# Moving the second copy of a hidden-layer chain and pair 0's attention in a hand-ordered two-layer graph kernel

## The chip, the cores and the metric

The kernel runs on one core of a Trainium2 chip. A core has a matrix engine (TensorE, PE in the profile), a vector engine (VectorE, DVE), an activation engine (ScalarE, ACT), a general engine (GpSimd, POOL) and a queue engine that issues DMA transfers (SyncE, SP). Each engine takes its own instructions in the order in which the program lists them, and waits at an instruction until its inputs are there. The metric is the device time of one execution in microseconds (us); lower is better.

## What is computed

There are 128 graphs of 128 nodes with 512 features each (`x`), and a 128 x 128 adjacency matrix for each graph (`adj`). Two layers follow, each with a residual and a layer norm. All arithmetic is float32. Cut to what matters:

```python
# layer 0: graph attention, 8 heads of 64 units
feats = einsum('bnf,hfu->bhnu', X, W)
e_self, e_neigh = feats . a_self, feats . a_neigh
dense = leaky_relu(e_self[..., :, None] + e_neigh[..., None, :], 0.2)
dense = dense + NEG_BIG * (1.0 - A)
att = softmax(dense)
x = layernorm(x + relu(att @ feats + b))
# layer 1: hypergraph convolution, 512 -> 1024 -> 512, twice
#   conv(x, W, b) = D^-1 H B^-1 H^T (x @ W^T) + b
h = layer_norm(relu(conv(x, W1, b1)), gamma, beta)
x = layernorm(x + conv(h, W2, b2) + x)
```

## The kernel before

The graphs are taken two at a time: 64 pairs, `p` = 0 to 63, with the two graphs `g` = 0 and 1 of a pair handled together. For the large products the kernel treats the two graphs and the two halves of the features as a 2 x 2 block matrix and forms it from seven half-size products instead of eight. `chain` (line 325 on) writes these out: products 1, 2, 6, 5, 7, 4, 3 in this order, into three PSUM banks called X, Y and W. Products 1, 6, 7 and 4 all add onto bank X, and its contents are needed at three stages, so ScalarE copies X out three times: copy 0 after product 1, copy 1 after product 6, copy 2 after product 7, ahead of product 4. A product that adds onto X can only start when the copy before it has read the bank. There are three such chains per pair: `pf` (attention features), `ph` (the hidden layer, 512 to 1024) and `py` (back to 512). The products of `ph` are at line 843 in the profile, those of `pf` and `py` at line 479, and all chain copies at line 335.

The order of all work is written by hand. Every step carries a due time. `at(lag, time, fn, ...)` and `@step(lag, time)` say that the step of pair `p` is due at `(p + lag) * T + time` with `T = 38.6`; the due times have no unit on the chip, they only order the program. A table `first` gives other due times for single steps of the first pairs, and a list `todo` holds the one-time preparations and pair 0's own steps. At the end everything is sorted by due time and issued in that order. So while one pair is in its `ph` chain (lag 3), the pair behind it is in its softmax (lag 2) and the one behind that in its feature products (lag 1).

ScalarE's part of that mixture matters here. In each period it runs, for the pair in the softmax, `leaky` (line 598, four instructions for half of one graph's heads) and `exponential` (line 612, likewise), and, for the pair ahead of it, the copies out of the `ph` chain. VectorE takes the row maximum between the two (`largest`, line 604), forms the sums of the chain (`h_sum`, line 858) and a skip term (`skip`, line 796). GpSimd does the mask (`masked`, line 582), the bias (`add_bias`, line 733), sums of blocks (`z_sums`, `h_sums`) and the power -0.5 of the variances (`rstds`, line 758).

Pair 0 goes through a prologue that differs from the other pairs. Its exponentials are transposed on TensorE (`e_transpose_first`, tile `pet`), evicted alternately by VectorE and ScalarE, and multiplied with the features by `attend` (line 670, tile `pav`), one block for each graph `g` and half of the heads `q`. `attended` (lines 706 and 707) divides by the softmax's denominator, `add_bias` adds the bias, `residual` (lines 742, 750 and 751) applies the relu, adds `x` and takes the statistics of a graph, `rstds` makes the inverse deviation from both graphs' statistics, and `first_shift` and `first_output` (lines 776 to 785) normalise. Only then can `propagate` (line 808, tile `pz`) start the second layer; it also needs `R`, which `r_evict` (line 443) makes. Besides, the prologue prepares weights: `prepare_hidden` (line 240) forms sums of 1024 columns for the hidden layer, three on GpSimd and one on VectorE. `prepare_output_spread` spreads one row over all partitions by a TensorE product (tile `gw`), and `prepare_output_blocks` (line 291, four instructions per block) scales the output weights with it on VectorE.

Of the kernel before, what the change touches and what calls it, by code (L numbers as in the profile page):

```python
# [20 lines left out]
def kernel(  # L21
# [45 lines left out]
    nc = tc.nc  # L67
# [21 lines left out]
    def bank(name):  # L89
        return psum.tile([P, HALF], F32, tag="bank", name=name)  # L90
# [223 lines left out]
    def at(lag, time, fn, *args, since=0, until=PAIRS):  # L314
        steps.append((lag, time, fn.__name__, range(since, until), fn, args))

    def chain(kind, lag, times, multiply, w, extra=0, since=0, until=PAIRS):

        tag = "chain" if w == HALF else "half"

        def product(p, s, i):
            where, start = {1: ("X", 1), 2: ("Y", 1), 6: ("X", 0), 5: ("W", 1), 7: ("X", 0),
                            4: ("X", 0), 3: ("W", 0)}[i]
            if start:
                s[kind, where] = bank(f"{kind}{where}_{p}")
            multiply(s, i, s[kind, where], start)  # L330

        def copy(p, s, i):
            n = w + (extra if i < 2 else 0)
            t = s[kind, i] = work.tile([P, HALF if w == HALF else FW], F32, tag=f"{tag}_{i}", name=f"{kind}{i}_{p}")
            nc.scalar.copy(t[:, :n], s[kind, "X"][:, :n])  # L335

        for i, t in zip((1, 2, 6, 5, 7, 4, 3), times):
            at(lag, t, product, i, since=since, until=until)
        for i, t in enumerate(times[7:]):
            at(lag, t, copy, i, since=since, until=until)  # L340
# [495 lines left out]
    def hidden(s, i, to, start):  # L836
# [4 lines left out]
        for m in range(KH // 2):  # L841
# [4 lines left out]
                    skip_group_check=True,  # L846
                )

    chain("ph", 3, (2.0, 3.8, 5.6, 7.35, 9.1, 12.65, 14.4, 4.0, 7.5, 11.0), hidden,
          HALF)  # L850

    def hid(s, g, q):
# [265 lines left out]
    for t, fn, *args in (  # L1118
# [21 lines left out]
        (15.46, load_weights, (nc.sync, w1_blocks[:1:-1], w1t, F // 2, HALF)),  # L1140
        (16.1, everywhere, (b2_bc, b2, nc.sync)),
        (79.0, prepare_hidden, (nc.gpsimd, 2)), (79.1, prepare_hidden, (nc.gpsimd, 0)),
        (79.2, prepare_hidden, (nc.gpsimd, 1)), (110.6, prepare_hidden, (nc.vector, 3)),
        (15.5, prepare_output_vectors, ()), (16.0, prepare_output, ()),
        (78.3, prepare_rows, ()), (78.79, prepare_output_sums, ()),
        (78.92, prepare_output_spread, (0, "gw")), (98.0, prepare_output_spread, (1, "bw")),
        (98.1, prepare_output_bias, ()), (98.2, prepare_output_blocks, (slice(0, 1),)),
        (99.75, prepare_output_blocks, (slice(1, 2),)),
        (117.8, prepare_output_blocks, (slice(2, 3),)),
# [14 lines left out]
        ("edges", 1): 110.4, ("scale_edges", 1): 110.5, ("neighbours", 1): 80.1,  # L1164
        ("propagator", 1): 117.76, ("spread_nodes", 1): 80.3, ("r_evict", 1): 121.8,
        ("leaky", 0, 1, 1): 77.65, ("leaky", 0, 0, 1): 73.6, ("largest", 0, 0, 1): 75.3,
        ("attend", 0, 0, 0): 78.95, ("attend", 0, 0, 1): 78.96, ("attend", 0): 97.85,
        ("attended", 0, 0): 99.7, ("attended", 0, 1): 99.8,
        ("leaky", 1, 0, 0): 117.85, ("leaky", 1, 0, 1): 117.9, ("leaky", 1, 1, 0): 119.9,
        ("largest", 1, 0, 0): 118.0, ("largest", 1, 0, 1): 118.2, ("largest", 1, 1, 0): 120.2,  # L1170
        ("masked", 1, 0, 0): 109.0, ("masked", 1, 1, 1): 121.5,
# [7 lines left out]
    for p, time, fn, *args in (  # L1179
        (0, 11.4, x_transpose_first), (0, 11.5, x_transpose_out, 0), (0, 11.5, x_transpose_out, 1),  # L1180
        (0, 12.5, plain_features, 0), (1, 12.55, x_transpose_first),
        (0, 12.6, plain_features, 1), (0, 12.65, adj_transpose_first),
        (0, 13.0, plain_features_out), (1, 13.1, x_transpose_out, 0), (1, 13.8, x_transpose_out, 1),
        (1, 14.5, plain_features, 0), (1, 14.6, plain_features, 1),
        (1, 15.6, plain_features_out), (1, 97.9, adj_transpose_first),
        (0, 78.8, e_transpose_first, 0, 0), (0, 78.85, e_transpose_first, 0, 1),
        (0, 78.9, e_transpose_first, 1, 0), (0, 79.3, e_transpose_first, 1, 1),
    ):
        todo.append((time, run, (fn, p, args)))
    for p in range(PAIRS):  # L1190
# [73 lines left out]
```

## Time and profile before

| | before |
|---|---|
| time, median of 3 runs | 2439.44 us (2438.86 to 2441.68) |
| span of the profiled execution | 2435.9 us |
| mean granted TensorE clock | 0.998 |
| TensorE matmul busy | 2408.6 us (99%) |
| VectorE busy | 1931.5 us (79%) |
| GpSimd busy | 1795.8 us (74%) |
| ScalarE busy | 1523.3 us (63%) |
| memory traffic | 140 GB/s over the span |

The span runs from the first to the last instruction; the time of a run is a little longer. Busy times are sums over instructions. A busy matmul engine is drawn with modelled ends, since matmuls overlap, so short gaps can disappear under them. In the lines of a timeline the first number is the start in us from the span's beginning, the second the length of a merged group of like instructions, then engine, source line, operation, output and inputs. A bracket at the end gives the idle time before the group and what is thought to have ended it. From about 90 us to 2380 us one pair follows another: the `propagate` products of consecutive pairs start 37.24 to 37.26 us apart from pair 2 on.

### The profile page before, as it was taken

The page shows a single profiled execution, that of the slowest core. Times are in us where ns is not written, and L with a number is a line of the kernel's source. Part 1 is how long each engine was busy: PE and PEld are TensorE (multiplying, and loading weights), DVE is VectorE, ACT ScalarE, POOL GpSimd, SP SyncE. Part 2 cuts the span into 40 slices and gives each one's busy share as a digit, 9 for nine tenths or more (in the row PEclk, how much of TensorE's full clock was granted, in tenths as well). Part 3 has the DMA queues.
Part 4 walks back from the last instruction along what each step waited for, and adds up shares of the span by engine and source line. Part 5 has one row for each costly group of instructions (what it writes and reads, how often), then busy time and mean ns, then how long its engine had stood idle before and what let it go on. Part 6 is the DMA issues. An engine that isn't in the chain of part 4 may idle for free.

```text
span 2435.9 us, 52769 instructions
## 1 busy us (share of the span) xinstructions
PE 2408.6 (99%) x18273; PEld 2148.9 (88%) x18273; DVE 1931.5 (79%) x4456; ACT 1523.3 (63%) x4481; POOL 1795.8 (74%) x2060
## 2 busy tenths in 40 slices
PE   7999999999999999999999999999999999999998
PEld 5898888998988988989989889889899898888897
DVE  7887788778878877887788788878877887887776
ACT  4665665765756656657557566576575675665763
POOL 5877777777777777777777777777777777777774
PEclk9999999999999999999999999999999999999999
DMA  6545545545455455454455555554544545545531
GB/s 185 140 145 146 146 136 148 153 131 150 138 142 149 143 145 147 134 155 141 133 147 148 140 145 147 145 147 131 157 137 135 153 140 145 144 142 150 147 110 53
DMA packets 432762, 345.30 MB, mean 142 GB/s; under 512 B 153176, under 2 KB 382064, under 8 KB 432496
## 3 DMA queue, kind: packets, MB, share of 16 engines
q1 hardware_dynamic: 429024, 337.46, 48.9%
q10 hardware_dynamic: 3472, 4.47, 0.6%
q8 instruction: 145, 2.38, 0.4%
q14 instruction: 121, 0.99, 0.1%
HBM read 239.08 MB, written 102.73 MB: 140 GB/s over the span
## 4 chain that ended last, share of the span: by engine, by line
PE 97%; DVE 1%; DMA 1%; ACT 1%; issue 0%; POOL 0%; SPq 0%; POOLq 0%; DVEq 0%; ACTq 0%
PE phX L843 19%; PE pyX L479 18%; PE phW L843 9%; PE pfX L479 9%; PE pyW L479 9%; PE pav L696 5%; PE pz L808 5%; PE phY L843 5%; PE pfW L479 5%; PE pq L1009 4%; PE pyY L479 4%; PE pfY L479 2%; PE pd L435 1%; PE pf L516 1%; PE py L1055 0%
## 5 line engine op out<-in xcount | busy, mean ns | idle before, releaser
L335 ACT COPY py<-pyX 128x257 f32<-128x257 f32 x189 | 70.9, 375 | 531.5 <-PE pyX L479 527.0
L843 PEld LDWEIGHTS phX<-zS,w_sb 128*128 128x128 f32 x3072 | 362.8, 192 | 41.5 <-issue 31.6
L843 PE MATMUL phX<-zS,w_sb 128*128 128x128 f32 x3072 | 378.9, 276 | 2.4 <-POOL xS L461 1.3
L896 POOL TENSOR_TENSOR sq<-sq 128x512 f32<-128x512 f32 (+2 forms) x384 | 326.4, 850 | 20.3 <-ACT sq L884 0.3
L582 POOL TENSOR_TENSOR nb<-nb,neg 128x512 f32<-128x512 f32 x256 | 318.0, 1275 | 7.6 <-DMA nb<-rd 7.2
L598 ACT ACTIVATE nb<-nb,ft 128x128 f32<-128x128 f32 x1020 | 317.3, 390 | 7.1 <-POOL nb L582 7.1
L758 POOL TENSOR_TENSOR rso<-veo,mhalf 128x2 f32<-128x2 f32 x63 | 44.1, 700 | 372.6 <-DVE veo L756 372.6
L612 ACT ACTIVATE nb<-nb,nm 128x128 f32<-128x128 f32 x1024 | 313.8, 394 | 0.4 <-DVE nm L604 0.4
L604 DVE TENSOR_REDUCE nm<-nb 128x4 f32<-128x512 f32 x256 | 172.5, 682 | 132.1 <-ACT nb L598 120.2
L873 ACT ACTIVATE h<-h,vecs 128x128 f32<-128x128 f32 x768 | 245.6, 395 | 34.6 <-DVE h L858 34.6
L479 PE MATMUL pyX<-w_sb,hS 128*128 128x257 f32 x1008 | 245.6, 385 | 0.0
L479 PE MATMUL pyX<-w_sb,h 128*128 128x257 f32 x1008 | 239.2, 379 | 0.5 <-ACT py L335 0.5
L479 PE MATMUL pyW<-w_sb,hS 128*128 128x256 f32 x1008 | 238.6, 378 | 1.0 <-DVE y L927 1.0
L479 PEld LDWEIGHTS pyX<-w_sb,h 128*128 128x128 f32 x1008 | 190.9, 190 | 29.0 <-ACT py L335 0.9
L479 PEld LDWEIGHTS pyW<-w_sb,hS 128*128 128x128 f32 x1008 | 190.6, 189 | 28.8 <-issue 1.4
L479 PEld LDWEIGHTS pyX<-w_sb,hS 128*128 128x128 f32 x1008 | 185.7, 189 | 28.7
L502 DVE TENSOR_TENSOR ft<-pf,pfW 128x264 f32<-128x264 f32 x124 | 53.3, 429 | 165.9 <-PE pfW L479 87.4
L633 DVE STREAM_TRANSPOSE eT<-eb 128x512 f32<-128x512 f32 x252 | 163.6, 687 | 2.5 <-DMA eb<-ed 2.1
L733 POOL TENSOR_TENSOR y<-y,b_bc 128x512 f32<-128x512 f32 x128 | 160.3, 1273 | 2.4 <-DVE y L707 1.1
L884 ACT ACTIVATE sq<-h 128x512 f32<-128x512 f32 x256 | 160.5, 628 | 2.1
L461 POOL TENSOR_TENSOR hS<-h 128x512 f32<-128x512 f32 x126 | 158.5, 1277 | 2.2 <-ACT h L873 2.2
L999 DVE SCALAR_TENSOR_TENSOR y<-y,rsh,bw_bc 128x512 f32<-128x512 f32 x126 | 148.3, 1215 | 11.7 <-POOL rsh L995 8.9
(178 smaller groups left out, 5687.7 us busy)
## 6 DMA issues: line engine op xcount, KB each, us to landing
nb<-rd SPq DMA_DIRECT2D x127, 512.0 KB
ed<-nb SPq DMA_DIRECT2D x126, 512.0 KB
eb<-ed SPq DMA_DIRECT2D x504, 128.0 KB
x<-in_x_dram SPq DMA_DIRECT2D x64, 512.0 KB
out_dram<-o SPq DMA_DIRECT2D x63, 512.0 KB
xb<-in_x_dram SPq DMA_DIRECT2D x248, 128.0 KB
a<-in_adj_dram SPq DMA_DIRECT2D x64, 128.0 KB
w<-in_adj_dram SPq DMA_DIRECT2D x128, 64.0 KB
```

Of the source, the lines that this page charges most:

```text
L461: engine.tensor_tensor(t[:, i], in0, in1, op=op)
L479: nc.tensor.matmul(to[:, :n], lhs[:, k, :], rhs[:, k, :n], start=bool(start) and k == 0, stop=(k == nk - 1), skip_group_check=True,)
L582: nc.gpsimd.tensor_tensor(t, t, neg[:, :, None, :].to_broadcast([P, NB, HH, B]), op=ALU.add)
L598: nc.scalar.activation(t, t, AF.Prelu, bias=s["ft"][:, g, h, 0:1], alpha=SLOPE)
L604: nc.vector.tensor_reduce(s["nm"][:, g, hs], scores(p, s, g, hs).rearrange("p b h j -> p h b j"), AX.XY, ALU.max, negate=True,)
L612: nc.scalar.activation(t, t, AF.Exp, bias=s["nm"][:, g, h:h + 1])
L633: nc.vector.transpose(s["eT"][:, g, hs, :].rearrange("p h (b i) -> p h b i", b=NB), s["eb", g][:, :, hs, :].rearrange("p b h j -> p h b j"),)
L733: nc.gpsimd.tensor_tensor(s["y"][:, g, :], s["y"][:, g, :], b0_bc, op=ALU.add)
L843: nc.tensor.matmul(to[:, m * N:(m + 1) * N], w[:, k, m * P:(m + 1) * P], rhs[:, k, :], start=bool(start) and m == 0 and k == 0, stop=(k == ...
L873: nc.scalar.activation(dst[:, k, :], src[:, k, :], AF.Relu, bias=b1_sb[:, c:c + 1])
L884: nc.scalar.activation(s["sq"][:, g, q * KH // 2:(q + 1) * KH // 2, :], hid(s, g, q), AF.Square, scale=DH ** -0.5,)
L896: nc.gpsimd.tensor_tensor(t[:, :n, :], t[:, :n, :], t[:, n:2 * n, :], op=ALU.add)
```

## The change

Three things are moved; no instruction is added or taken away.

The first edit is in the `ph` chain and so in every pair. Copy 1 is due at 5.95 in place of 7.5. The next pair's `leaky` for its second graph and second half of the heads is due at 6.0, so on ScalarE the copy now precedes it.

The second concerns TensorE, ScalarE and VectorE in the prologue. Pair 0's fourth transpose comes before the attention products, these follow for both graphs in a row, and the product that spreads `gw` comes behind them. The division, bias, residual and statistics of both graphs are due together, and the inverse deviation right after them. The second weight block and `R` come behind that.

The third is on GpSimd: the second sum of the hidden weights (`prepare_hidden` with index 1) is due after pair 0's two bias additions in place of before them.

The purpose is to have the copy that product 7 waits for done before other ScalarE work of another pair, and to bring pair 0's two graphs to the second layer side by side.

```diff
-    chain("ph", 3, (2.0, 3.8, 5.6, 7.35, 9.1, 12.65, 14.4, 4.0, 7.5, 11.0), hidden,
+    chain("ph", 3, (2.0, 3.8, 5.6, 7.35, 9.1, 12.65, 14.4, 4.0, 5.95, 11.0), hidden,
           HALF)
...
-        (79.2, prepare_hidden, (nc.gpsimd, 1)), (110.6, prepare_hidden, (nc.vector, 3)),
+        (98.0, prepare_hidden, (nc.gpsimd, 1)), (110.6, prepare_hidden, (nc.vector, 3)),
...
-        (78.92, prepare_output_spread, (0, "gw")), (98.0, prepare_output_spread, (1, "bw")),
+        (78.99, prepare_output_spread, (0, "gw")), (98.0, prepare_output_spread, (1, "bw")),
...
-        ("attend", 0, 0, 0): 78.95, ("attend", 0, 0, 1): 78.96, ("attend", 0): 97.85,
-        ("attended", 0, 0): 99.7, ("attended", 0, 1): 99.8,
+        ("attend", 0, 0, 0): 78.95, ("attend", 0, 0, 1): 78.96, ("attend", 0, 1, 0): 78.97,
+        ("attend", 0, 1, 1): 78.98, ("attended", 0, 0): 97.8, ("attended", 0, 1): 97.81,
+        ("add_bias", 0, 0): 97.82, ("add_bias", 0, 1): 97.83,
+        ("residual", 0, 0): 99.6, ("residual", 0, 1): 99.65, ("rstds", 0, "a"): 99.7,
...
-        (0, 78.9, e_transpose_first, 1, 0), (0, 79.3, e_transpose_first, 1, 1),
+        (0, 78.9, e_transpose_first, 1, 0), (0, 78.93, e_transpose_first, 1, 1),
```

## The prediction, made before the changed kernel ran

> **What bounds the kernel now.** I read the page first: the engine that is busy all the time, and the chain that ended last.
>
> ```profile
> PE 2408.6 (99%) x18273; PEld 2148.9 (88%) x18273; DVE 1931.5 (79%) x4456; ACT 1523.3 (63%) x4481; POOL 1795.8 (74%) x2060
> ...
> PE 97%; DVE 1%; DMA 1%; ACT 1%; issue 0%; POOL 0%; SPq 0%; POOLq 0%; DVEq 0%; ACTq 0%
> ```
>
> TensorE sets the end, so a faster helper engine is worth only what it takes out of TensorE's waits. Its idle time is 2435.9 - 2408.6 = 27 us, nearly all before 90 us and after 2380 us. But the change moves something in every pair, so I next read the timeline of one middle pair, TensorE first, then ScalarE.
>
> ```profile
> 1028.51 1.95 PE L843 MATMUL phX<-zS,w_sb 128*128 128x128 f32 x16
> 1030.30 1.95 PE L843 MATMUL phW<-zS,w_sb 128*128 128x128 f32 x16
> 1032.22 2.02 PE L843 MATMUL phX<-zS,w_sb 128*128 128x128 f32 x16
> 1034.08 1.89 PE L1009 MATMUL pq<-y,R 128*128 128x512 f32 x4
> ...
> 1027.99 2.45 ACT L612 ACTIVATE nb<-nb,nm 128x128 f32<-128x128 f32 x8
> 1030.34 1.27 ACT L598 ACTIVATE nb<-nb,ft 128x128 f32<-128x128 f32 x4
> 1031.51 0.57 ACT L335 COPY ph<-phX 128x512 f32<-128x512 f32 x1
> 1031.97 2.45 ACT L612 ACTIVATE nb<-nb,nm 128x128 f32<-128x128 f32 x8
> 1034.32 0.58 ACT L335 COPY ph<-phX 128x512 f32<-128x512 f32 x1
> ```
>
> The columns are start, length and group. From product 6 (1028.51) to product 5 (1030.30) is 1.79 us, as between any two full products here. From product 5 to product 7 it is 1.92. Product 7 adds onto bank X, which the second copy reads, and that copy ends at 1031.51 + 0.57 = 1032.08; product 7 starts 0.14 later. TensorE was ready at 1030.30 + 1.785 = 1032.085. So product 7 seems to wait 0.135 to 0.14 us for the copy's signal, in every pair. Going through the timeline pair by pair, the distance is 1.92 or 1.93 in all of pairs 1 to 62 (62 times). The last pair has no attention work left on ScalarE, and is the control:
>
> ```profile
> 2403.75 1.95 PE L843 MATMUL phW<-zS,w_sb 128*128 128x128 f32 x16
> 2405.53 1.95 PE L843 MATMUL phX<-zS,w_sb 128*128 128x128 f32 x16
> ...
> 2403.95 0.59 ACT L335 COPY ph<-phX 128x512 f32<-128x512 f32 x1 [3.21 <-PE phX L843]
> ```
>
> There the copy ends at 2404.54, early, and the distance is 1.78. In pair 0 product 7 starts at 62.30, again 0.71 after the copy's start at 61.59, as in the middle pair (1032.22 - 1031.51). So this is a wait, though the page books it as nothing.
>
> Third, the prologue, from the timelines and the windows view.
>
> ```profile
> 39.32 2.37 POOL L240 TENSOR_TENSOR w_sb<-w_sb 128x1024 f32<-128x1024 f32 x1
> 44.15 1.64 POOL L733 TENSOR_TENSOR y<-y,b_bc 128x512 f32<-128x512 f32 x1 [1.14 <-DVE y L707]
> 45.76 0.40 POOL L369 TENSOR_SCALAR neg<-a 128x256 f32<-128x256 f32 x1
> ...
> 45.82 0.88 DVE L742 SCALAR_TENSOR_TENSOR y<-y,x 128x512 f32<-128x512 f32 x1 [0.21 <-POOL y L733]
> 47.68 0.17 DVE L756 TENSOR_SCALAR vea<-mva 128x2 f32<-128x2 f32 x1
> ...
> 49.92 3.64 PE L808 MATMUL pz<-R,y 128*128 128x128 f32 x16 [7.18 <-ACT y L785]
> 65.58 2.02 PE L843 MATMUL phX<-zS,w_sb 128*128 128x128 f32 x16 [1.25 <-POOL xS L461]
> ...
> 63.73 1.28 ACT L612 ACTIVATE nb<-nb,nm 128x128 f32<-128x128 f32 x4 [0.40 <-DVE nm L604]
> 64.92 0.56 ACT L335 COPY ph<-phX 128x512 f32<-128x512 f32 x1
> ...
> 48.00:50.00 2.00, 0.08 (x1) 0.08 (x1) 1.90 (x8) 1.32 (x4) 2.00 (x3) 0.50 0.05 7
> ```
>
> TensorE waits 7.18 us for pair 0's normalised rows, then again at 65.58. That second wait is named for GpSimd, but product 4 follows the third copy of X: 64.92 + 0.56 = 65.48, plus about 0.1. That copy stands behind four exponentials, these behind the maximum that VectorE takes at 63.02. And VectorE is busy almost without a break from 38.33 to that maximum (18.82 of the 20 us from 40 to 60). VectorE, not TensorE, sets when pair 0 gets through.
>
> **What the Trainium skill says.** Perfetto Trace Analysis, "Tensor Engine Instruction (MATMUL, LD_WEIGHTS)": a matmul's reported end is estimated, and the travel of a semaphore is outside the window. The trace agrees: product 5 is drawn until 1032.25, past the start of its successor, so a 0.14 us bubble lies under a modelled tail. GPSIMD Engine Reference, "Key points": GpSimd shares its SBUF interfaces with VectorE and contends with instructions that have two SBUF inputs. The trace agrees: the residual at 45.82 ends 0.54 us after GpSimd's 0.40 us mask does (46.70, 46.16), where the one before it took 0.68 in all. So I treat a GpSimd instruction as holding such a VectorE instruction off until it ends. TensorE: Matmul & The Clock Gate, "What's actually happening": after an idle window of about 3.4 us the clock is halved, until it has been busy about as long. Here it stopped at 42.74 and shows 0.50 from 48 to 53.
>
> **Part 1, the second copy at 5.95 in place of 7.5.** In ScalarE's order it jumps ahead of the four leaky activations of the next pair, second graph, second half (due 6.0 of lag 2). Nothing is added or removed. The copy can start when the exponentials are out (1030.34) and product 6 has drained (1028.51 + 1.95 = 1030.46): 1030.5, ending 1031.05 instead of 1032.08. TensorE's 1032.085 is then 1 us away, and the wait goes: 62 x 0.14 = 8.7 us.
>
> The price: ScalarE now waits about 0.15 us for product 6, and behind the copy stand the leaky activations (0.6 later), eight exponentials (0.15 later) and the third copy. The third copy ends near 1035.05; product 4, due at 1035.66, hides it by 0.5. The last maximum on VectorE moves from 1031.89 to about 1032.2, and with it the sum over W (1035.88 to 1036.2, done by 1036.8), which must be read before product 3 at 1037.45: hidden by 0.6. VectorE stands idle 1.3 us at each feature sum, which absorbs the rest. The exponentials' write to DRAM leaves 0.15 later; the transposes that read it back find it early (only 2.1 us of waits on it in the run, 3 times). One of these 3 is the last pair's second graph, where VectorE and then TensorE (0.36 us at 2385.61) wait for it on the chain to the end. So pair 62 gains nothing and 0.15 is lost: 8.7 - 0.14 - 0.15 = 8.4 us.
>
> **Part 2, the prologue.** The fourth transpose of pair 0 goes ahead of attention, all four attention blocks follow it, then the gw row. TensorE: fourth transposes from 37.3 (exponentials end 37.15) to 37.8; attention at 0.54 each, to 40.0; gw ready at 41.1 (before: 38.3). VectorE: attended 0 from 38.5 to 39.6, attended 1 to 40.7 (before 41.0 and 44.0), 0.45 idle for gw, first weight block 41.15 to 42.7 (1.57). GpSimd: the second weight sum (2.37 us, at 39.32 above) moves behind both biases: bias 0 from 39.65 to 40.9, bias 1 to 42.2, weight sum to 44.55. Residual 0 is ready at 42.7, but it has two SBUF inputs, so I let it wait for the weight sum: 44.55. Then 1.6 us for each graph's residual and statistics: the variance at 47.9, against 47.68. Without the hold it would be 46.05. From the variance to pz is 2.24 us (49.92 - 47.68): pz at about 50.1. The second weight block (1.56) and R (0.33) that now follow the variance end at 49.8, just before y, so R delays nothing. DRAM row loads behind dnb start some 5 us later but are used after 57 us.
>
> From there VectorE has the same work as before, 1.9 us of it moved behind the variance. Its three two-port or two-input steps (hB twice, the last weight sum) again queue behind GpSimd's three masks, now 49.2 to 52.95; the last mask decides. I get the next maximum at 55.75 against 55.45, so product 4 and all behind it are 0.3 later. Moving copy 1 in pair 0 lets product 7 start near 60 instead of 62.3, and TensorE then only waits longer at product 4. Part 2: +0.3 us; if residual 0 is not held, the same steps give -1.5.
>
> **Sum.** 2439.44 - 8.4 + 0.3 = 2431.3 us.
>
> **Rivals.**
> A. Prologue also gains: residual 0 slips in ahead of the weight sum. For it: only 0.5 us decide. Against: the wait for gw. 2439.44 - 8.4 - 1.5 = 2429.5.
> B. The 0.14 us is eaten by another wait, at product 4, product 3 or a feature copy, whose slacks I read as 0.5, 0.6 and 0.3 us. For it: TensorE fed by three busy engines. Against: all three are at least twice the 0.14 us. Then 2439.44 + 0.3 = 2439.7, no change.
> C. Slower: the later maximum pushes VectorE's sums into TensorE by some 0.1 us per pair, 62 x 0.1 = 6.2, with the prologue's 0.3: 2446. Against: the idle 1.3 us twice per pair on VectorE.
>
> **How the numbers follow.** Forecast 0.60, A 0.24, B 0.10, C 0.06. The first two are faster by over 0.2% (4.9 us), and a partly eaten gain is too: 0.86. B gives most of same, 0.08; C slower, 0.06. The range takes in A with the scatter of the runs below (2428.6) and above the forecast a halved clock after the longer wait at product 4, or a quarter of the gain lost: 2434.6.
>
> **What would show it.** Product 5 to product 7 at 1.79 in all middle pairs, the pitch of pairs 37.25 to 37.11; the second copy straight behind the exponentials, with a short wait on TensorE. In the prologue: both attended groups done by 41, residual 0 starting late with a length near 2.4 us (right) or at 0.7 (rival A), pz near 50.1, product 4 near 65.9. I am wrong if the pitch stays at 37.25, whoever is then named.

## The result and the profile after

The changed kernel takes 2428.53 us (median of 4 runs, 2427.39 to 2428.98), beside 2439.93 for the kernel before: a ratio of 0.9952, with a 95% interval of [0.9935, 0.9969] (brackets behind a ratio are this interval from here on). The forecast was 2431.3, its range 2428.6 to 2434.6. So the direction was right, the time lies 0.07 us below the range, and the gain of 10.9 us against the forecast's 2439.44 came out a third larger than the 8.1 foreseen. The profiled span went from 2435.9 to 2425.6, that is by 10.3.

TensorE still sets the end. First the page of the kernel before, three groups that the prediction did not read: a line, an operation with count, then busy time and mean length, then the idle time ahead of it.

```profile
L843 PEld LDWEIGHTS phX<-zS,w_sb 128*128 128x128 f32 x3072 | 362.8, 192 | 41.5 <-issue 31.6
L843 PE MATMUL phX<-zS,w_sb 128*128 128x128 f32 x3072 | 378.9, 276 | 2.4 <-POOL xS L461 1.3
...
L999 DVE SCALAR_TENSOR_TENSOR y<-y,rsh,bw_bc 128x512 f32<-128x512 f32 x126 | 148.3, 1215 | 11.7 <-POOL rsh L995 8.9
```

The page of the changed kernel:

```profile
PE 2398.0 (99%) x18273; PEld 2140.8 (88%) x18273; DVE 1947.1 (80%) x4456; ACT 1519.0 (63%) x4481; POOL 1795.3 (74%) x2060
...
L843 PEld LDWEIGHTS phX<-zS,w_sb 128*128 128x128 f32 x3072 | 363.0, 192 | 33.0 <-issue 30.4
L843 PE MATMUL phX<-zS,w_sb 128*128 128x128 f32 x3072 | 374.3, 275 | 2.4 <-POOL xS L461 2.4
...
L999 DVE SCALAR_TENSOR_TENSOR y<-y,rsh,bw_bc 128x512 f32<-128x512 f32 x126 | 148.2, 1214 | 31.7 <-POOL rsh L995 31.4
```

Two things went and one came. The weight loads of products 6, 7 and 4 wait 41.5 - 33.0 = 8.5 us less: 62 times 0.137, the wait that the prediction found. Their matmuls are also busy 378.9 - 374.3 = 4.6 us less, 62 times 0.074, though not one of them was removed or made smaller: this the prediction did not foresee. And VectorE now waits 31.4 us in place of 8.9 for GpSimd's `rsh`, which has to do with a third term of the sum, taken up below.

The timeline of a middle pair after, TensorE and then ScalarE:

```profile
1024.74 1.95 PE L843 MATMUL phX<-zS,w_sb 128*128 128x128 f32 x16
1026.53 1.95 PE L843 MATMUL phW<-zS,w_sb 128*128 128x128 f32 x16
1028.31 1.95 PE L843 MATMUL phX<-zS,w_sb 128*128 128x128 f32 x16
1030.10 1.89 PE L1009 MATMUL pq<-y,R 128*128 128x512 f32 x4
...
1026.72 0.59 ACT L335 COPY ph<-phX 128x512 f32<-128x512 f32 x1
1027.21 1.28 ACT L598 ACTIVATE nb<-nb,ft 128x128 f32<-128x128 f32 x4
1028.39 2.45 ACT L612 ACTIVATE nb<-nb,nm 128x128 f32<-128x128 f32 x8
```

Copy 1 now precedes `leaky` and ends at 1027.31, a full microsecond before product 7. From product 5 to product 7 it is 1.78 (before 1.92), as forecast. From product 7 to `pq` it is 1.79 (before 1034.08 - 1032.22 = 1.86), and product 7 itself is drawn 1.95 long in place of 2.02.

The distance between the starts of consecutive groups, as a mean over pairs 2 to 61, accounts for the pitch, which is the distance from one pair's `pz` to the next pair's (worked out from the traces of both kernels, in us):

| from - to | before | after | difference |
|---|---|---|---|
| product 5 to product 7 (`ph`) | 1.925 | 1.787 | -0.138 |
| product 7 to `pq` | 1.860 | 1.787 | -0.073 |
| product 6 to product 5 (`pf`) | 0.890 | 0.912 | +0.022 |
| product 1 to product 2 (`ph`) | 1.787 | 1.799 | +0.012 |
| product 2 to product 6 (`pf`) | 0.890 | 0.892 | +0.002 |
| whole pitch | 37.254 | 37.080 | -0.175 (from means not rounded) |

Over the 60 pitches from pair 2 to pair 62 that is 10.47 us. Up to `pz` of pair 2 it takes 0.29 longer (128.90, before 128.61), and the last pitch is 32.33 in place of 32.48. So 0.29 - 10.47 - 0.15 = -10.33, the whole difference of the spans. The medians lie 0.6 us further down than that (10.9), less than the 2.8 us over which the runs of the kernel before scatter.

The prologue, GpSimd, VectorE and TensorE:

```profile
42.55 2.35 POOL L240 TENSOR_TENSOR w_sb<-w_sb 128x1024 f32<-128x1024 f32 x1
...
42.85 2.59 DVE L742 SCALAR_TENSOR_TENSOR y<-y,x 128x512 f32<-128x512 f32 x1
46.30 0.66 DVE L742 SCALAR_TENSOR_TENSOR y<-y,x 128x512 f32<-128x512 f32 x1
47.94 0.17 DVE L756 TENSOR_SCALAR vea<-mva 128x2 f32<-128x2 f32 x1
...
50.17 3.78 PE L808 MATMUL pz<-R,y 128*128 128x128 f32 x16 [7.52 <-ACT y L785]
66.03 2.02 PE L843 MATMUL phX<-zS,w_sb 128*128 128x128 f32 x16 [2.42 <-POOL xS L461]
```

Residual 0 is held until 0.54 us after GpSimd's weight sum (45.44 and 44.90), the variance comes at 47.94 (forecast 47.9), `pz` at 50.17 (50.1), product 4 at 66.03 (65.9).

These times count from the start of the span, and what comes ahead of the moved steps does not take the same time in every execution. ScalarE's first copy of transposed exponentials, which stands ahead of them, starts 0.30 us later in the changed kernel's profile, first before, then after:

```profile
37.15 0.56 ACT L645 COPY eT<-pet 128x512 f32<-128x512 f32 x1
```

```profile
37.45 0.57 ACT L645 COPY eT<-pet 128x512 f32<-128x512 f32 x1
```

From that copy to product 4 it is 28.43 us before and 28.58 after; in `copy_only`, which has the old prologue, 28.63, and in `prologue_only`, which has the new one, 28.29. So no effect of the prologue on product 4 can be told from this scatter.

### The profile page after: what moved, and what is told of

It reads as the page before. It is cut to its first block, busy times and chain, and to the rows that moved or that the text cites. A ratio compares the mean times of both kernels' runs of the same rounds, so it can differ in the third digit from the quotient of the medians.

```text
span 2425.6 us, 52771 instructions
## 1 busy us (share of the span) xinstructions
PE 2398.0 (99%) x18273; PEld 2140.8 (88%) x18273; DVE 1947.1 (80%) x4456; ACT 1519.0 (63%) x4481; POOL 1795.3 (74%) x2060
## 4 chain that ended last, share of the span: by engine, by line
PE 97%; DVE 1%; DMA 1%; issue 0%; POOL 0%; ACT 0%; SPq 0%; POOLq 0%; DVEq 0%; ACTq 0%
PE pyX L479 18%; PE phX L843 18%; PE pfX L479 9%; PE phW L843 9%; PE pyW L479 9%; PE pav L696 5%; PE pz L808 5%; PE phY L843 5%; PE pfW L479 5%; PE pq L1009 4%; PE pyY L479 4%; PE pfY L479 2%; PE pd L435 1%; PE pf L516 1%; PE py L1055 0%
## 5 line engine op out<-in xcount | busy, mean ns | idle before, releaser
L843 PE MATMUL phX<-zS,w_sb 128*128 128x128 f32 x3072 | 374.3, 275 | 2.4 <-POOL xS L461 2.4
L999 DVE SCALAR_TENSOR_TENSOR y<-y,rsh,bw_bc 128x512 f32<-128x512 f32 x126 | 148.2, 1214 | 31.7 <-POOL rsh L995 31.4
```

Of the source, the lines that this page charges most:

```text
L843: nc.tensor.matmul(to[:, m * N:(m + 1) * N], w[:, k, m * P:(m + 1) * P], rhs[:, k, :], start=bool(start) and m == 0 and k == 0, stop=(k == ...
```

## The experiments

**Each part alone.** From the kernel before, only copy 1 moved; from the changed kernel, copy 1 put back.

```diff
# copy_only: the kernel before, with
-    chain("ph", 3, (2.0, 3.8, 5.6, 7.35, 9.1, 12.65, 14.4, 4.0, 7.5, 11.0), hidden,
+    chain("ph", 3, (2.0, 3.8, 5.6, 7.35, 9.1, 12.65, 14.4, 4.0, 5.95, 11.0), hidden,
# prologue_only: the changed kernel, with
-    chain("ph", 3, (2.0, 3.8, 5.6, 7.35, 9.1, 12.65, 14.4, 4.0, 5.95, 11.0), hidden,
+    chain("ph", 3, (2.0, 3.8, 5.6, 7.35, 9.1, 12.65, 14.4, 4.0, 7.5, 11.0), hidden,
```

> The kernel before with the second copy of the ph chain at 5.95 and nothing else. Theory (the whole gain is the copy's; each removed wait gives back 0.14 us ahead of product 7 and a further 0.07 us behind it, less about 0.035 of new waits): pitch of the pairs 37.08 against 37.25, profiled span shorter than before by 60 x 0.175 + 0.15 = 10.6 us, a little more than with the full change, since product 4 of pair 0 stays near 65.6. Rival (the prologue brings the part that the prediction missed): only 8.4 us shorter, pitch 37.11.

> The changed kernel with the second copy back at 7.5. Theory: pitch 37.25 again, residual 0 still about 2.6 us long, product 4 of pair 0 near 66.0; span within 0.6 us of before, if anything longer (+0.3). Rival (the prologue brings 2 us or more): 2 us shorter than before.

The copy alone: 2430.49 us (2429.92 to 2432.29), ratio 0.9961 [0.9948, 0.9973], pitch 37.075. The pitch is the theory's, not the rival's 37.11. But the profiled span is only 6.8 us shorter than before (2429.1), not 10.6: TensorE waits 2.47 us at product 4 of pair 0, its clock is halved for 3.4 us from 68.3 on, and from pair 0's `pz` to pair 1's it takes 44.28 us (before 41.17, changed kernel 41.38).

The prologue alone: 2440.82 (2439.21 to 2443.46), ratio 1.0002 [0.9994, 1.001]. Its pitch is 37.254 apart from one pair, in which product 7 waited 1.2 us longer; product 7 to `pq` is back at 1.860. The profiled span, 2439.0, was to stay within 0.6 us of before and is 3.1 longer, of which 1.24 is that one wait and 1.44 the later start (38.59 in place of 37.15 at the copy above); the medians differ by 0.4.

The two steps of the table belong to the copy and go together. The prologue's edits bring nothing by themselves. With the early copy they may bring 1.4 to 2 us, since the copy alone is slower than the whole change in every run and its pair 0 takes longer; but the two intervals overlap and the kernels were not timed side by side, so this is not shown.

**A longer wait.** Copy 1 later still, behind the exponentials that follow.

```diff
-    chain("ph", 3, (2.0, 3.8, 5.6, 7.35, 9.1, 12.65, 14.4, 4.0, 7.5, 11.0), hidden,
+    chain("ph", 3, (2.0, 3.8, 5.6, 7.35, 9.1, 12.65, 14.4, 4.0, 7.85, 11.0), hidden,
```

> The kernel before with the second copy of ph at 7.85, so that it stands behind four more exponentials (1.17 us). Theory (product 7 waits for the copy, and whatever the length of the wait, the product that waited takes a fixed 0.07 us longer because its first weights were not loaded ahead): product 5 to product 7 grows from 1.92 to 3.1 us, product 7 to pq stays at 1.86; pitch 37.25 + 1.17 = 38.4, about 72 us longer. Rival (the 0.07 grows with the wait, or the 0.14 us has nothing to do with the copy): product 7 to pq over 1.9, or the distance stays near 1.92.

2518.67 us (2 runs), ratio 1.0321 [1.0302, 1.034], pitch 38.42. Its timeline:

```profile
1032.77 2.02 PE L843 MATMUL phX<-zS,w_sb 128*128 128x128 f32 x16 [1.15 <-ACT ph L335]
1034.63 1.89 PE L1009 MATMUL pq<-y,R 128*128 128x512 f32 x4
```

Product 5 to 7 is now 3.10 (1029.67 to 1032.77), a wait of 1.31. Yet product 7 to `pq` is 1.86, exactly as after the wait of 0.14. So at product 7 the 0.07 is a price of having waited at all, whatever the length. The weight loads show where it arises, first before, then after:

```profile
1032.19 1.86 PEld L843 LDWEIGHTS phX<-zS,w_sb 128*128 128x128 f32 x16
1033.97 0.30 PEld L1009 LDWEIGHTS pq<-y,R 128*128 128x128 f32 x2
```

```profile
1028.20 1.87 PEld L843 LDWEIGHTS phX<-zS,w_sb 128*128 128x128 f32 x16
1029.99 0.30 PEld L1009 LDWEIGHTS pq<-y,R 128*128 128x128 f32 x2
```

After, the first load of product 7 begins 0.11 ahead of its matmul (1028.20, 1028.31), as that of `pq` does in both kernels (1033.97, 1034.08). Before, it begins 0.03 ahead (1032.19, 1032.22): it waited too, and the first matmul then runs at the pace of its own load. The Trainium skill (TensorE: Matmul & The Clock Gate, "Step-by-step: what each phase is for") says that TensorE pulls the next weights' load ahead of running matmuls; these lines agree, and show that a wait forfeits that lead, of some 0.08 us.

**Is residual 0 really held?** GpSimd's second weight sum behind the variance.

```diff
-        (98.0, prepare_hidden, (nc.gpsimd, 1)), (110.6, prepare_hidden, (nc.vector, 3)),
+        (99.72, prepare_hidden, (nc.gpsimd, 1)), (110.6, prepare_hidden, (nc.vector, 3)),
```

> The changed kernel with GpSimd's second weight sum due at 99.72, behind the inverse deviation, in place of 98.0. Theory (the weight sum holds residual 0 off): residual 0 falls from 2.59 to about 0.7 us, pz starts near 48.3 in place of 50.17; of these 1.9 us some 0.8 arrive at product 4 of pair 0 (65.2 against 66.03), because the masks now stand behind the weight sum; span about 0.8 us shorter than with the change. Rival (VectorE's amount of work sets product 4 whatever the order): pz earlier, product 4 within 0.2 us of 66.0, span the same.

```profile
44.23 0.68 DVE L742 SCALAR_TENSOR_TENSOR y<-y,x 128x512 f32<-128x512 f32 x1
45.77 0.66 DVE L742 SCALAR_TENSOR_TENSOR y<-y,x 128x512 f32<-128x512 f32 x1
47.41 0.17 DVE L756 TENSOR_SCALAR vea<-mva 128x2 f32<-128x2 f32 x1
```

With the same inputs the residual takes 0.68 in place of 2.59. The Trainium skill (GPSIMD Engine Reference, "Key points") speaks of contention with VectorE instructions that have two SBUF inputs; here it was a hold until GpSimd's instruction had ended (residual 0 at 45.44, the weight sum at 44.90). From residual 0 to `pz` it is 49.65 - 44.23 = 5.42 us, in place of 7.32: the 1.9 us that the prediction put on the hold. Product 4 starts at 66.43, and ScalarE's first copy, from which it was counted above, at 38.76: 27.67 us between them in place of 28.58, and 27.67 again in `best2` below, which has this edit too. So a gain of about the theory's 0.8 us does arrive there. But the time is 2431.65 (2427.16 to 2433.91), ratio 0.9964 [0.995, 0.9978]: no time is gained. Product 4 waits 2.46 us, and the windows view (PE, PEld, DVE, ACT, POOL, the clock, DMA) shows what follows:

```profile
64.00:66.00 2.00, 0.00 (x0) 0.00 (x0) 1.44 (x3) 1.42 (x5) 2.00 (x3) 0.99 0.50 156
66.00:68.00 2.00, 1.57 (x7) 1.60 (x8) 1.64 (x2) 2.00 (x8) 2.00 (x2) 0.50 1.07 311
68.00:70.00 2.00, 2.00 (x14) 2.00 (x13) 1.25 (x1) 1.29 (x5) 1.92 (x2) 0.65 0.17 66
```

The clock is halved for 3.4 us and product 4 lasts 3.44 in place of 2.02; at 93.3 us, behind a wait of 2.30, it is halved once more. From pair 0's `pz` to pair 1's it is 46.25 us in place of 41.38. The other runs fit: the one of 2427.16 us had a mean granted clock of 0.998, the four of 2431.64 to 2433.91 us had 0.996.

**The third term: what holds the pitch at 37.08.** Without any wait of the middle pairs it would be 37.254 - 0.138 - 0.073 = 37.043. The theory: a closed loop over VectorE and GpSimd now has TensorE's own length. In it, `rsa`, `rsh` and `rso` are the inverse deviations (`rstds`) of the first layer's norm, the hidden norm and the output norm, and `veo` is the output's variance. `rsa` on GpSimd releases the masks, then come the sums `zS` and `rsh`; VectorE's `y_scale` (line 999) waits for `rsh`, and behind it stand `largest`, `skip`, `scale_edges` (tile `hB`), the sums and `veo`; GpSimd's `rso` waits for `veo`, and squares, hidden sums and biases follow, which lead to the next pair's `rsa`. VectorE in the changed kernel:

```profile
1026.29 2.34 DVE L999 SCALAR_TENSOR_TENSOR y<-y,rsh,bw_bc 128x512 f32<-128x512 f32 x2 [0.59 <-POOL rsh L995]
...
1030.88 0.47 DVE L426 TENSOR_SCALAR hB<-hT,deg 128x128 f32<-128x128 f32 x2
...
1036.04 0.17 DVE L756 TENSOR_SCALAR veo<-mvo 128x2 f32<-128x2 f32 x1
```

First a longer loop: a sum of 128 x 256 on VectorE ahead of `veo`.

```diff
+    def extra(p, s):
+        nc.vector.tensor_tensor(spare, b0_bc[:, :QU], b2_bc[:, :QU], op=ALU.add)
+    at(4, 15.55, extra, until=LAST)
```

> The changed kernel with one VectorE sum of 128x256 (about 0.34 us from start to start) added just before the output's variance of each pair. Theory (the VectorE and GpSimd loop is the bound): the pitch grows by the whole 0.34 us, to about 37.4, some 20 us longer than with the change. Rival (TensorE is the bound and the loop has room): pitch 37.08 to 37.1, less than 2 us longer.

2438.77 us (2437.2 to 2441.74), ratio 0.9995 [0.9987, 1.0003], pitch 37.232. The whole gain is gone, by one VectorE instruction on an engine that is 80% busy. The growth, 0.15, lies between the theory's 0.34 and the rival's next to nothing: the distance from the statistics' last step (the aggregate, line 751) to `veo` grew only from 0.22 to 0.41 us, so the sum partly fills a pause that was there already. Taking that 0.19 off 37.232 leaves a loop of 37.04.

Then a shorter loop. In `nodes_later` the adjacency's row operation (line 351) was put elsewhere, and `best` combined that with two edits of the prologue.

```diff
# nodes_later (best: also the sum above and pair0_split below)
-    @step(0, 11.0)
+    @step(0, 21.35)
...
-    @step(0, 17.0)
+    @step(0, 21.36)
```

> The changed kernel with the row sums of the adjacency (nodes) due at 21.35 in place of 11.0, so that VectorE does them in its idle time ahead of a feature sum, and not between the second layer's scaling and the output's variance. Theory (after the change a closed loop of VectorE and GpSimd work sets the pitch of 37.08, since TensorE alone would need 37.25 - 0.14 - 0.07 = 37.04): the loop gets some 1.3 us of room, the small waits at the feature chain's product 6 and the hidden chain's product 1 go, pitch 37.04, 60 x 0.037 = 2.2 us shorter than with the change. Rival (the 0.037 us comes from ScalarE, whose copies are late because the second copy now waits for product 6): pitch stays at 37.07 to 37.08.

> The changed kernel with three of these edits together: copy 1 of pair 0 at 7.5, the weight sum at 99.72, the row sums at 21.35. Theory: the gains add, 0.8 + 2.2 us and the clock that is not halved: about 2425 us, 3 to 4 us below the change. Rival (only the order in the prologue matters): 2427 to 2428.

2625.12 us (1.0756 [1.0731, 1.0782]) and 2622.68 (1.0744 [1.073, 1.0759]). The operation now stood ahead of the sum that reads bank W of `pf`. The line of TensorE's groups in `nodes_later` says it: 122.2 us of waiting, 2 us in each of 60 pairs.

```profile
L479 PE MATMUL pfW<-w_sb,xS 128*128 128x264 f32 x496 | 142.8, 413 | 122.2 <-DVE ft L502 122.2
```

Two things made it so dear. At its new place the operation stands beside GpSimd's sums, and its two-input instructions take four times as long, first in the changed kernel, then in `nodes_later`:

```profile
L351 DVE SCALAR_TENSOR_TENSOR w<-a,w 128x128 f32<-128x128 f32 x128 | 31.5, 281 | 0.0
```

```profile
L351 DVE SCALAR_TENSOR_TENSOR w<-a,w 128x128 f32<-128x128 f32 x128 | 139.1, 1121 | 0.0
```

This fits the hold seen at residual 0. And 42 of the 60 waits were followed by a halved clock, for 3.4 us each time; the pitch is 40.9 us where that happened and 39.3 where it did not.

These two runs say nothing about the loop. The next one moved `hB` (0.4 us) from ahead of `veo` to just behind it.

```diff
-    @step(1, 10.8)
+    @step(1, 15.65)
     def scale_edges(p, s):
```

> The changed kernel with the scaling of the edges (scale_edges, two VectorE instructions, 0.4 us) due at 15.65 in place of 10.8, so that it comes behind the output's variance and out of the VectorE and GpSimd loop; nothing of it touches a PSUM bank. Theory (after the change this loop, at about 37.04 us, stands level with TensorE's own 37.04, and the two together give 37.08): with 0.4 us of room the small waits at the feature chain's product 6 and the hidden chain's product 1 go (0.89 and 1.79 us again), pitch 37.04 to 37.05, 1.5 to 2 us shorter than the change. Rival (those waits come from ScalarE's copy waiting for product 6): pitch stays at 37.07 to 37.08, product 6 at 0.91 to 0.92.

```profile
1029.88 2.35 DVE L999 SCALAR_TENSOR_TENSOR y<-y,rsh,bw_bc 128x512 f32<-128x512 f32 x2
...
1039.33 0.17 DVE L756 TENSOR_SCALAR veo<-mvo 128x2 f32<-128x2 f32 x1
1039.41 0.48 DVE L426 TENSOR_SCALAR hB<-hT,deg 128x128 f32<-128x128 f32 x2
```

`y_scale` to `veo` is 9.45 us in place of 9.75, and `y_scale` has no wait here any more (10.8 us in the whole run in place of 31.7). The pitch is 37.044 with hardly a deviation, the `pf` step is back at 0.890 and the `ph` one at 1.787. ScalarE's order is as in the changed kernel, so the third term comes from the loop and not from that order. How much two such level periods lose to each other is not fixed, though: in the profile of `pair0_split` below, which leaves `hB` in its place, the pitch is 37.052. Why it is less there stays open. But the time of `edges_later` is 2430.3 (2429.64 to 2432.19), ratio 0.9961 [0.9948, 0.9973]: from pair 0's `pz` to pair 1's it takes 44.9 us in place of 41.4, by these waits, of which the changed kernel has only the last, with 1.05 us.

```profile
76.23 1.13 PE L479 MATMUL pfX<-w_sb,xS 128*128 128x264 f32 x4 [1.29 <-ACT pf L335]
80.69 1.13 PE L479 MATMUL pfW<-w_sb,xS 128*128 128x264 f32 x4 [0.69 <-DVE ft L502]
94.82 1.97 PE L479 MATMUL pyW<-w_sb,hS 128*128 128x256 f32 x8 [2.13 <-DVE y L927]
```

**Pair 0's two waits.** With copy 1 early, TensorE's two waits of pair 0 (1.15 at product 7, 1.25 at product 4) merge into one of 2.42. Here they are kept apart, by leaving pair 0's copy at its old place.

```diff
+            if p == 0 and (lag, time) == (3, 5.95):
+                time = 7.5
```

> The changed kernel with the second copy of ph back at 7.5 for pair 0 alone. Theory (in pair 0 the moved copy gathers TensorE's two waits of about 1.2 us into one of 2.4 us, after which the clock is halved in some executions): waits of about 1.1 and 1.3 us, the clock at 1.00 from 58 to 74 us in the profile, median as the changed kernel's best or up to 1 us below its median, and the runs closer together. Rival (the clock has nothing to do with where the wait lies): times and scatter as with the change.

2428.61 us (2427.88 to 2429.65), ratio 0.9954 [0.9941, 0.9966], waits of 0.75 and 1.27: no difference to the change in time, against the theory. It could hardly show one, since the changed kernel's profile has no halved clock at its wait of 2.42 us. In the profile the smaller pitch, 37.052, was paid for at the start: from pair 1's `pz` to pair 2's it takes 39.05 us in place of 37.35.

**Towards a better version.** `best2` is the split, the later sum and the later `hB` together; `edges_from4` the later `hB` from pair 4 on; `best3` that and the split.

```diff
# edges_from4 and best3, beside the edit of edges_later
+        ("scale_edges", 2): 126.6, ("scale_edges", 3): 165.2,
```

> The changed kernel with the weight sum at 99.72, copy 1 of pair 0 at 7.5, and the scaling of the edges at 15.65. Theory: pz of pair 0 some 1.9 us earlier than with the change, TensorE's waits in pair 0 split in two and the clock kept, pitch 37.04 to 37.05: about 2425.5 us, 3 us below the change. Rival (scatter of the start-up covers it): 2427 to 2429.

> The later hB from pair 4 on; pairs 2 and 3 keep their order. Loop theory: pitch 37.044 from pair 4 on, and if it was the moved hB of pairs 2 and 3 that cost the 3.5 us at the start, the first pairs go as with the change (pair 0's pz to pair 1's near 41.4). Then 60 x 0.035 = 2.1 us off the change: span near 2423.5, time near 2426.5, ratio about 0.9943. Rival: the start-up waits come from something else, pair 0 to 1 stays near 44.9 and the time near 2430.

> edges_from4 with pair 0's copy 1 left at its old place. The two edits touch different stages, so if pair 0's split is worth nothing by itself (2428.61 beside 2428.53), this equals edges_from4 within the scatter, 2426.5; if the split keeps the TensorE clock from being halved in some executions, it is the tighter of the two, with a range of runs under 2 us.

`best2`: 2430.18 (2428.7 to 2430.78), 0.9957 [0.9943, 0.997], with the start-up waits of `edges_later` and a halved clock at 93.9 us. `edges_from4`: 2428.87 (2426.02 to 2431.18), 0.9955 [0.9941, 0.9968]. `best3`: 2427.15 (2425.95 to 2427.83), 0.9945 [0.9933, 0.9958]. In both of the last the pair 0 to 1 distance is back at 41.4 and the pitch is 37.04 to 37.05, so it was the `hB` of pairs 2 and 3 that spoiled the start. The five runs of `edges_from4` fall into 2426.0 to 2426.2, 2428.9, and 2430.9 to 2431.2; those of `best3` stay within 1.9 us. The profile of `best3` has the two short waits:

```profile
63.55 2.02 PE L843 MATMUL phX<-zS,w_sb 128*128 128x128 f32 x16 [1.04 <-ACT ph L335]
66.84 2.02 PE L843 MATMUL phX<-zS,w_sb 128*128 128x128 f32 x16 [1.28 <-POOL xS L461]
```

The one of `edges_from4` that was profiled has a single wait of 2.46 us and kept its clock. Its two longest executions had a mean granted clock of 0.995, the two shortest 0.997, and the one between them 0.996. So a clock that is halved for longer goes with the longer time; at which wait is not shown, as none of the longer ones has a trace. `best3` is the fastest kernel of the study by its median; its interval and that of the change overlap, and they were not timed side by side, so that it beats the change is likely, not shown.

## Why the prediction was right or wrong

- **The wait at product 7** was real, there in all pairs from 1 to 62, and it went: 1.92 to 1.79. The one-microsecond slack of the copy, the third copy, the later maximum and the sum over W came much as worked out. Measured from product 6, the maximum starts 0.43 later than before (3.81 us behind product 6 in place of 3.38), forecast some 0.3, and was hidden.
- **The step that failed is the term "62 x 0.14 = 8.7 us"**: the mechanism was right, its size was not. It counted the gap ahead of product 7 and not what the gap does to product 7 itself, 0.073 us more. With it a pair gains 0.211, not 0.14. The evidence stood in the lines shown: product 7 had 2.02 us where every other full product had 1.95, and its distance to `pq` was 1.86. The forecast read the starts ahead of the wait and not those behind it.
- **A part was eaten, as in rival B but smaller**: 0.036 us of the 0.211 in each pair, by the VectorE-GpSimd loop. The slacks of 0.3 to 0.6 us that the forecast checked were those of single copies and sums against TensorE; none of them shows that a loop of other engines has the same period. Together: 0.175 in place of 0.14 per pair, 10.5 us over 60 pairs in place of 8.4.
- **The tail** was to give 0.14 + 0.15 back, as pair 62 was to gain nothing. The wait for the last pair's `eT` did grow, from 0.36 to 0.45 us, but the last pitch became 0.15 shorter. This is 0.3 us more of gain.
- **The prologue**: the hold on residual 0 is shown, and `sum_after` gives its size, 1.9 us. The small differences look right (+0.26 at the variance, +0.25 at `pz`, +0.45 at product 4 where 0.3 was forecast, +0.29 for pair 2), but this is in part luck: the changed kernel's profile began 0.30 us later, and the kernel before and `copy_later`, whose prologue is the same up to there, lie 2.2 us apart at `pz` (49.92 and 52.09). That the prologue is worth about nothing was right; that it costs 0.3 is not shown. Rival A (residual slips in) did not happen; that its time was nearest is chance. Rival C did not happen.
- **The range** reached down only to rival A, and held no allowance for a gain per pair larger than the gap. The miss of 0.07 us is far inside the scatter of the runs; what counts is the gain of the middle pairs, forecast 2.1 us too small, because every unknown in it was taken to cut one way.

## What to carry to other kernels

To price a wait of the engine that sets the end, compare start-to-start distances on both sides of it with those of an equal group that didn't wait; here the gap was 0.14 us, and its price 0.21. Once a wait is gone from every iteration, ask which closed loop of the other engines comes next, by walking once around it: two engines 80% and 74% busy had a loop just as long as TensorE's own period. And where the first iteration differs from the rest, leave an edit out of it and look at it apart: what gained 0.036 us in each of 60 pairs cost 3.5 us at the start.

## What was not expected of the hardware

- A wait of TensorE at product 7 cost 0.07 us beyond itself, whether 0.14 or 1.31 us long, and the waits of 2 us at bank W in `nodes_later` cost the same (0.297 us from the first matmul to the second in place of 0.223). It is not the same everywhere: in `loop_longer` product 1 of `ph` starts 0.07 us late and then takes 0.10 more.
- The clock was halved after some single waits of 2.0 to 2.5 us and not after others: after 42 of 60 in `nodes_later` (2.0 to 2.1 us), in `sum_after` (2.46) and in `copy_only` (2.47), but not in the changed kernel (2.42) or in `edges_from4` (2.46). The Trainium skill (TensorE: Matmul & The Clock Gate, "What's actually happening") gives an idle window of about 3.4 us for this; these runs show it after less. In these three runs the clock stayed halved for 3.41 us each time. No wait of 0.75 to 1.3 us brought it, among them 60 of 1.15 us in `copy_later`.
- VectorE instructions with two SBUF inputs took far longer beside GpSimd's sums: 2.59 us in place of 0.68 for residual 0, 1.12 in place of 0.28 for the adjacency's row operation.
- An extra VectorE instruction inside a dependent chain lengthened it by only 0.19 us, as it partly filled the 0.22 us between the aggregate's start and `veo`.
